# Row sums of one head of four, in two query chunks of every odd attention step, taken on VectorE instead of ScalarE

## The chip, the cores and the metric

One core of a Trainium2 chip runs the whole kernel. The metric is the device time of one execution in microseconds. The kernel before took 660.53 us (median of 3 runs, 660.41 to 660.67).

## The reference

The input `x` is (8, 512, 512): 8 batches of 512 tokens with 512 features. There are 16 heads of 32 features. A conditioning token per batch goes through the same projections and is added to the queries and keys, and the attention's output is added to `x`:

```python
Q = split_heads(x @ Wq.T + bq)
K = split_heads(x @ Wk.T + bk)
V = split_heads(x @ Wv.T + bv)
tQ = split_heads(tokens @ Wq.T + bq)
tK = split_heads(tokens @ Wk.T + bk)
scores = einsum('bhqd,bhkd->bhqk', Q + tQ, K + tK) / sqrt(32)
attn = softmax(scores, axis=-1)
out = einsum('bhqk,bhkd->bhqd', attn, V)
return x + out            # heads put side by side again
```

Everything is in float32. A softmax row needs its largest score, the exponentials of the 512 scores less that largest one, and the sum of these exponentials. This sum, one number for each query and head, is what the change is about.

## The kernel before

**Steps.** A step `t` is one batch and one group of four heads: 8 batches with 4 groups give 32 steps. The 512 queries (and keys) are four chunks of 128. The main loop (L1133) runs over steps 1 to 28; the first step and the last three are written out ahead of it and behind it.

**Two kinds of steps.** Weighting the values needs exponentials with the keys on the partitions. The row maxima and row sums are made with the queries on the partitions.

- In *odd* steps 1 to 27 (`BLOCKED`, L76) the exponentials that are made query-wise for the sums are kept. `denominators` (L679) writes them into eight rooms of a ring called `arena` (`rows_kept`, L222), four rooms for the first two query chunks and four for the other two. In a room the four heads of a chunk stand side by side, so one head of one chunk is four pieces of 128 columns, one in each of four rooms. `exchange` (L668) moves them between partitions by DMA, 16 transfers for each half (12 from SP's queue, 4 from GpSimd's), into `blocks`. `turn_blocks` (L661) transposes them on VectorE in 32x32 blocks. They are then keyed and go straight into the weighted sum (`times_v`, L765).
- In *even* steps the query-wise exponentials are thrown away (written back over the scores in PSUM), only their sums are kept, and `exponentials` (L744) makes the scores again key-wise, with the row maximum subtracted by a first matmul (L749), and then the exponentials (L763, ScalarE) into the other rooms of `arena`.

**One pass of the loop.** Step `t` has four items, called V, q, k and v. In each item

1. if `t` is even, `exponentials(t, i)` makes the keyed exponentials of key chunk `i`: matmuls L749 and L752, then four ScalarE instructions L763;
2. `row_max` (L606) makes the scores of a query chunk of the *next* step, four heads, each in a PSUM bank (matmuls L646, or L638 in odd steps), and VectorE takes their maxima (L602 for one head, L655 for two). In items V, q and k these are chunks 1, 2 and 3 of step `t + 1`; in item v it is chunk 0 of step `t + 2`;
3. `denominators` (L679) makes the four exponentials of that chunk on ScalarE (L693), one for each head, with the row maximum as bias. Each also asks for the sum of what it makes (`accum_out`). The profile shows such a sum as an instruction of its own behind the exponential, an ACTIVATION_READ_ACCUMULATOR on the same line;
4. the item's own product: in V the weighted sum of step `t - 1` (L774), in q, k and v part of the projections of the next batch (matmuls L469). The projections are multiplied block by block in seven products instead of eight. In even steps an item makes three of the seven (`three_products`, L547), and VectorE adds them up in three instructions, L556, L557 and L558, straight out of two PSUM banks. In odd steps an item makes four of them (`four_products`, L517), which ScalarE (L540 to L543) and GpSimd (L544, L545) take up.

So the query-wise exponentials of an odd step are made one step earlier, in the even one: chunk 1 in item V, chunk 2 in item q, chunk 3 in item k.

**Order and banks.** Each engine's order is written out by hand: a manual schedule takes the instructions of an engine in the order in which the code names them. PSUM has eight banks. `released` (L144) writes down, item by item, which of them come free in which order, and `begin` (L137) hands them out again. In an even step the scores of an item go into four banks: two that held scores of the item before, free when ScalarE has made the exponentials from them, and two that held its product, free when VectorE has done L557 and L558. In item k, for example, the scores L646 wait for the third and fourth head's exponentials of item q and for L557 and L558 of item q.

**Where the sums go.** `masked` (L794, GpSimd L801) takes a step's sums in that step's own item k, TensorE spreads them over the partitions (L811), and VectorE takes reciprocals (L821) that scale the weighted values.

Of the kernel before, what the change touches and what calls it, by code (L numbers as in the profile page):

```python
# [12 lines left out]
ALU = mybir.AluOpType  # L13
AX = mybir.AxisListType
# [3 lines left out]
def kernel(  # L18
# [38 lines left out]
    nc = tc.nc  # L57
# [14 lines left out]
    EARLY = 3  # L72
    SINGLY = "qk"
    BY_POOL = (3,)
    WARM = (48, 4)
    BLOCKED = list(range(1, T - 4, 2))  # L76

# [44 lines left out]
    def banks(i, n=1):  # L122

        row = row_of[0] or [at_end[j] for j in TURNS[turn[0]]]
        j = row[i]
        if n == 1:
            return psum[:, j, :]
        k = row[i + 1]
        return psum[:, j : k + 1 : k - j, :]
# [7 lines left out]
    def begin(w):  # L137
        rows = order[w : w + 4]
        pairs = [(j, j + 1) for j in rows if j + 1 in rows]
        last = max(pairs, key=lambda p: rows.index(p[0]) + rows.index(p[1]), default=sorted(rows[2:]))  # L140
        order[w : w + 4] = sorted(j for j in rows if j not in last) + list(last)
        row_of[0] = list(order)

    def released(*roles):  # L144
        order[:] = [row_of[0][i] for i in roles]
# [76 lines left out]
    def rows_kept(t, half):  # L222

        a = arena[:, half * HG : (half + 1) * HG, :]
        return a.rearrange("p g (c h s) -> p g c h s", c=2, h=HG)
# [368 lines left out]
    sums = {}  # L594
# [66 lines left out]
    def turn_blocks(t, units):  # L661

        for n in units:
            pr = slice(n % NP * 2, n % NP * 2 + 2)
            e = blocked[t][:, :, n // NP, pr, :].rearrange("p g h s -> p g (h s)")
            nc.vector.transpose(e, e)  # L666

    def exchange(t, half):  # L668
# [3 lines left out]
        for g in range(HG):  # L672
            for a in range(HG):
                queue = nc.gpsimd if a in BY_POOL else nc.sync
                of = arena[a * BL : (a + 1) * BL, half * HG + g, :]
# [3 lines left out]
    def denominators(t, qc, w=HG, js=range(HG)):  # L679

        if t >= T - 2:
            return
        for j in js:
            if t in BLOCKED:
                to = rows_kept(t, qc // 2)[:, :, qc % 2, j, :].rearrange(
                    "p g (c e) -> p g c e", e=BL
                )
            else:
                to = banks(w + j)
            of = banks(w + j)  # L690
            if t in BLOCKED:
                of = of.rearrange("p (c g e) -> p g c e", g=HG, e=BL)
            nc.scalar.activation(  # L693
                to,
                of,
                AF.Exp,
                bias=nmax[t][:, qc, j, :],
                accum_out=sums[t][:, qc, j, :],
            )

    def split_max(t, on=nc.gpsimd):

        if t >= T or t in BLOCKED:
            return
        m, sp = nmax[t], split[t % 2]
        rest = op.tile([P, NS, HG, 1], F32, tag="rest", name=f"rest_{t}")
        on.tensor_copy(sp[:, :, :, 0:1], m)
        on.tensor_tensor(rest, m, sp[:, :, :, 0:1], ALU.subtract)
        on.tensor_copy(sp[:, :, :, 1:2], rest)
        on.tensor_tensor(sp[:, :, :, 2:3], rest, sp[:, :, :, 1:2], ALU.subtract)  # L710
# [7 lines left out]
    def turn_max(t):  # L718

        if t >= T or t in BLOCKED:  # L720
            return
        maxT[t] = room_for_max(t)
        nc.sync.dma_start_transpose(
            maxT[t].rearrange("p (c q) -> p c q", c=NS),
            split[t % 2].rearrange("p c h e -> p (c h e)"),
        )
# [17 lines left out]
    def exponentials(t, kc, at=None):  # L744

        bank = [bank_of(i) for i in at] if at else [banks(i) for i in range(HG)]
        for j in range(HG):
            r = slice(j * HD, j * HD + 3)
            nc.tensor.matmul(bank[j], onesb[r, :], maxT[t][r, :], start=True, stop=False)  # L749
        for j in range(HG):  # L750
            r = slice(j * HD, (j + 1) * HD)
            nc.tensor.matmul(  # L752
                bank[j],
                qkT["k", t][r, kc * P : (kc + 1) * P],
                qkT["q", t][r, :],
                start=False,
                stop=True,
            )
        for pr in range(NP):
            e = room_for_e(t, kc, pr)  # L760
            es[t, kc, pr] = e
            for i in range(2):
                nc.scalar.activation(e[:, i, :], bank[pr * 2 + i], AF.Exp)  # L763
# [145 lines left out]
    def keep_warm(n):  # L909
        for _ in range(n):  # L910
            nc.tensor.matmul(warm[:, :P], onesb, onesb, start=True, stop=True)

    keep_warm(WARM[0])
    bank = bank_of
# [5 lines left out]
    def turn_first_x(half):  # L920
        if half == 0:
            xT[0] = xtp.tile([P, NC, S], F32, tag="xT", name="xT_0")
        for cs in ((slice(0, 1), slice(1, 2)) if half else (slice(0, 2),)) + (slice(2, 4),):
            nc.vector.transpose(
                xT[0][:, cs, two[half]].rearrange("p c (f i) -> p c f i", i=BL),
                x0[:, half_of_x[half], cs, :].rearrange("p f c e -> p c f e"),
            )

    def project(t, n, pt, at=slice(0, S)):
        for cc in range(NC):  # L930
            project_qk_part(t, n, cc, pt, at)
# [5 lines left out]
    project(0, "k", pk, two[0])  # L937
    keep_warm(WARM[1])
    turn_first_x(1)
# [156 lines left out]
    def products(t, n, blocks, hold, dens, small):  # L1096

        b, r = (t - 1) // G + 1, (t - 1) % G
        hold()
        if r % 2:  # L1100
            three_products(n, b, r // 2, dens, small, (0, 3))
            released(1, 2, 4, 5, 6, 7, 0, 3)
        elif blocks:
            four_products(n, b, r // 2, dens, small, 4)
            released(6, 7, 0, 1, 2, 3, 5, 4)
        else:
            four_products(n, b, r // 2, dens, small, 0)
            released(2, 3, 4, 5, 6, 7, 1, 0)
# [5 lines left out]
    def turn_more(t, i):  # L1114

        for u in (t - 1, t, t + 1):
            if u in BLOCKED and (t - u, i) in TURNED:
                n = turned.get(u, 0)
                turned[u] = n + TURNED[t - u, i]
                turn_blocks(u, range(n, turned[u]))  # L1120

    ORDERS = {
        (1, 0): [],
        (1, 1): ["store", "x"],
# [8 lines left out]
    for t in range(1, T - 3):  # L1133
        b, r = divmod(t, G)
        blocks = t in BLOCKED
        w = 0 if blocks else HG
        items = ["V", "q", "k", "v"]
        for i, item in enumerate(items):
            rows = (t + 1, i + 1) if i < 3 else (t + 2, 0)
            begin(w)  # L1140
            if not blocks:
                exponentials(t, i)
            late_first = item in ("v" if blocks else "qkv") and t % 2 == 1
            hold = row_max(*rows, late_first, w, not blocks and item in SINGLY)

            def held(i=i, hold=hold):
                hold()
                if i == 2:
                    split_max(t + 1)
                    turn_max(t + 1)  # L1150

            dens = lambda js=range(HG): denominators(*rows, w, js)
            if item in "qkv":
                products(t, item, blocks, held, dens, nothing)
            else:
                held()
                dens()
                if blocks:
                    weighted(t - 1, banks(4), banks(5), nothing)
                    released(6, 7, 0, 1, 2, 3, 5, 4)  # L1160
                else:
                    weighted(t - 1, banks(0), banks(1), nothing)
                    released(2, 3, 1, 4, 5, 6, 7, 0)
            if i == 0 and r % 2 == 0:
                turn_x(t + NC + 2)
                turn_x(t + NC + 3)
            if i == 0 and r == 1:
                combine_x(b + 1, 1, nc.gpsimd)
            if i == 1 and r == 0:
                combine_x(b + 1, 0, nc.gpsimd)  # L1170
            if i == 2:
                aparts[t] = masked(t)
            turn_more(t, i)
            for what in ORDERS[t % 2, i]:
                if what == "store":
                    store()
                elif what == "residual":
                    if 3 < t + 1 <= T - 4:
                        load_residual(t + 1)
                elif what == "x":  # L1180
                    load_pairs()
                elif t + 1 in BLOCKED:
                    exchange(t + 1, what)
# [67 lines left out]
    t = T - 3  # L1251
# [25 lines left out]
    t = T - 2  # L1277
# [25 lines left out]
    t = T - 1  # L1303
# [117 lines left out]
```

## Time and profile before

| | |
|---|---|
| median of 3 runs | 660.53 us (660.41 to 660.67) |
| the profiled execution's own time | 660.98 us |
| its span, first to last instruction | 658.9 us |
| TensorE busy | 651.5 us, granted clock 1.00 |
| VectorE busy | 574.6 us |
| ScalarE busy | 542.5 us |
| GpSimd busy | 336.8 us |
| query-wise exponentials that are kept (L693) | 224, with 224 reads of the accumulator |
| query-wise exponentials that are not kept (L693) | 256, with as many reads |

The profile is of one execution. PE is TensorE's matmuls, PEld its weight loads, DVE is VectorE, ACT ScalarE, POOL GpSimd and SP the engine that only issues DMAs. In rows in order of time the columns are start, duration, engine, line, operation, the tile written and the tile read, shapes, how many instructions were merged into the row, and, in square brackets, how long the engine stood idle before it and what ended that. In rows of groups they are line, engine, operation, tiles, shapes and count, then busy time and mean duration in ns of one, then the idle time before them. Instructions of one engine overlap a little: the next starts before the end of the last is written, so the distance between two starts is shorter than a duration. A float32 matmul is two passes with a weight load each, so one row of scores for four heads is eight matmuls.

### The profile page before, as it was taken

Reading aid. Unit: us, or ns where it says so; the run is one execution under the profiler, and the core shown is the slowest. Engines: PE = TensorE matmul, PEld = TensorE weight load, DVE = VectorE, ACT = ScalarE, POOL = GpSimd, SP = SyncE. Lnnn points to the kernel's source line nnn. Section 1 sums busy time; section 2 is a strip of 40 time slices with the busy share of each in tenths; the row PEclk is TensorE's granted clock in tenths of the full one; section 3 lists DMA queues with packets and bytes.
Section 4 is the critical chain, followed back from the end, with each engine's and each line's share of the span. In section 5 each row is a group of like instructions: output and inputs, shape, how many; then the busy total and the mean of one; then the engine's idle time right before and its main releaser. Section 6 shows DMA issues by size and latency. Waiting matters only on the chain.

```text
span 658.9 us, 23947 instructions
## 1 busy us (share of the span) xinstructions
PE 651.5 (99%) x9568; PEld 304.1 (46%) x9568; DVE 574.6 (87%) x844; ACT 542.5 (82%) x1393; POOL 336.8 (51%) x446
## 2 busy tenths in 40 slices
PE   8999999999999999999999999999999999999997
PEld 7444443544535454444445444454553544444432
DVE  4898989989798898979989898898979888897886
ACT  2579798888989888898989979788897988889664
POOL 5552543647537464466635664464753646444340
PEclk9999999999999999999999999999999999999999
DMA  9718548385675838657484875839567582940212
GB/s 205 144 44 214 118 109 210 67 220 122 153 172 121 209 74 214 149 130 194 94 214 97 191 155 131 210 71 217 118 164 166 115 205 48 223 106 4 56 33 33
DMA packets 140818, 90.91 MB, mean 138 GB/s; under 512 B 117436, under 2 KB 126308, under 8 KB 140708
## 3 DMA queue, kind: packets, MB, share of 16 engines
q1 hardware_dynamic: 133252, 73.91, 49.0%
q0 software_dynamic: 5568, 14.95, 8.8%
q8 instruction: 75, 1.23, 0.8%
q10 hardware_dynamic: 1888, 0.52, 0.4%
q14 instruction: 35, 0.29, 0.1%
HBM read 20.27 MB, written 8.39 MB: 43 GB/s over the span
## 4 chain that ended last, share of the span: by engine, by line
PE 95%; POOL 2%; DVE 1%; DMA 1%; issue 0%; ACT 0%; ACTq 0%; DVEq 0%; POOLq 0%
PE psum L469 43%; PE psum L774 17%; PE psum L646 10%; PE psum L638 9%; PE psum L752 8%; PE psum L749 3%; PE psum L410 2%; DMA early<-in_x_dram 1%; PE psum L1227 1%; PE psum L1340 0%; PE psum L811 0%; ACT psum L693 0%; POOL wc_q L364 0%; POOL wc_q L361 0%; POOL wc_k L362 0%
## 5 line engine op out<-in xcount | busy, mean ns | idle before, releaser
L602 DVE TENSOR_REDUCE nmax<-psum 128x1 f32<-128x512 f32 x326 | 204.9, 680 | 41.7 <-PE psum L646 38.2
L693 ACT ACTIVATE psum<-psum,nmax 128x512 f32<-128x512 f32 x256 | 169.2, 665 | 46.5 <-DVE nmax L602 34.3
L763 ACT ACTIVATE arena<-psum 128x512 f32<-128x512 f32 x264 | 136.3, 603 | 29.3 <-PE psum L752 21.7
L693 ACT ACTIVATE arena<-psum,nmax 128x512 f32<-128x512 f32 x224 | 152.8, 709 | 5.8 <-issue 4.4
L666 DVE STREAM_TRANSPOSE blocks<-blocks 128x1024 f32<-128x1024 f32 x112 | 132.2, 1218 | 0.2 <-issue 0.2
L655 DVE TENSOR_REDUCE nmax<-psum 128x2 f32<-128x1024 f32 x87 | 105.3, 1212 | 1.1 <-PE psum L646 1.1
L842 POOL TENSOR_TENSOR res<-res,recs 128x512 f32<-128x512 f32 x30 | 31.4, 1048 | 121.1 <-DVE res L841 121.1
L677 POOL DMA_DIRECT2D blocks<-arena x112 | 55.9, 504 | 72.3 <-ACT arena L693 63.5
L646 PE MATMUL psum<-kT,qT 32*128 32x512 f32 x576 | 87.9, 604 | 0.0
L774 PE MATMUL psum<-arena,v 128*32 128x512 f32 x576 | 68.5, 597 | 0.0
L752 PE MATMUL psum<-qT,kT 32*128 32x512 f32 x528 | 67.9, 587 | 0.0
L638 PE MATMUL psum<-kT,qT 32*64 32x512 f32 x896 | 62.4, 613 | 0.0
L646 PEld LDWEIGHTS psum<-kT,qT 32*128 32x128 f32 x576 | 37.6, 182 | 34.1 <-DVE kT L558 6.5
L693 ACT ACTIVATION_READ_ACCUMULATOR psum<-psum,nmax 128x1 f32 x256 | 52.4, 205 | 0.0
L774 PE MATMUL psum<-blocks,v 128*32 128x256 f32 x896 | 52.1, 381 | 0.0
L693 ACT ACTIVATION_READ_ACCUMULATOR arena<-psum,nmax 128x1 f32 x224 | 50.9, 227 | 0.0
L843 POOL TENSOR_TENSOR xr<-res,xr 128x512 f32<-128x512 f32 x30 | 38.4, 1281 | 2.4
L209 POOL TENSOR_TENSOR xr<-xr,wT_q 128x512 f32<-128x512 f32 x30 | 38.3, 1280 | 0.3
L774 PEld LDWEIGHTS psum<-blocks,v 128*32 128x32 f32 x896 | 26.3, 110 | 25.0 <-ACT arena L763 10.6
L841 DVE STREAM_TRANSPOSE res<-psum 128x512 f32<-128x512 f32 x28 | 20.1, 717 | 19.0 <-issue 16.0
L469 PE MATMUL psum<-wT_v,xT 128*32 128x256 f32 x512 | 34.2, 382 | 0.0
L469 PE MATMUL psum<-wc_v,xc 128*32 128x256 f32 x512 | 33.5, 379 | 0.0
(194 smaller groups left out, 1012.3 us busy)
## 6 DMA issues: line engine op xcount, KB each, us to landing
blocks<-arena SPq DMA_DIRECT2D x336, 128.0 KB, 4.1
blocks<-arena POOLq DMA_DIRECT2D x112, 128.0 KB, 4.0
xr<-in_x_dram SPq DMA_DIRECT2D x60, 128.0 KB, 2.8
x<-in_x_dram SPq DMA_DIRECT2D x56, 128.0 KB, 2.8
out_dram<-xr SPq DMA_DIRECT2D x56, 128.0 KB, 2.3
w_q<-in_L_cond_Wq_dram SPq DMA_DIRECT2D x4, 256.0 KB
w_k<-in_L_cond_Wk_dram SPq DMA_DIRECT2D x4, 256.0 KB, 8.2
w_v<-in_L_cond_Wv_dram SPq DMA_DIRECT2D x4, 256.0 KB
```

Source lines behind the costliest of these rows:

```text
L469: nc.tensor.matmul(pt[r], still[:, r], moving, start=(kc == kcs[0]), stop=(kc == kcs[-1]))
L602: nc.vector.tensor_reduce(nmax[t][:, qc, j : j + 1, 0], pt, AX.X, ALU.max, negate=True)
L638: nc.tensor.matmul(pt[i * n : (i + 1) * n], qkT["q", t][r, qc * P + i * n : qc * P + (i + 1) * n], qkT["k", t][r, :], start=True, stop=True,)
L646: nc.tensor.matmul(pt, qkT["q", t][r, qc * P : (qc + 1) * P], qkT["k", t][r, :], start=True, stop=True,)
L655: nc.vector.tensor_reduce(nmax[t][:, qc, pr * 2 : pr * 2 + 2, 0], pt, AX.X, ALU.max, negate=True)
L666: nc.vector.transpose(e, e)
L677: queue.dma_start(to.rearrange("p c h s -> p (c h s)"), of)
L693: nc.scalar.activation(to, of, AF.Exp, bias=nmax[t][:, qc, j, :], accum_out=sums[t][:, qc, j, :],)
L752: nc.tensor.matmul(bank[j], qkT["k", t][r, kc * P : (kc + 1) * P], qkT["q", t][r, :], start=False, stop=True,)
L763: nc.scalar.activation(e[:, i, :], bank[pr * 2 + i], AF.Exp)
L774: nc.tensor.matmul(pt[j * HD : (j + 1) * HD, at], vs[b % 2][:, kc, (g * HG + j) * HD : (g * HG + j + 1) * HD], e, start=(kc == chunks[0]), ...
L843: nc.gpsimd.tensor_tensor(xr[t], y, xr[t], ALU.add)
```

## The change

For steps 3 to 27 (odd), the exponentials of head 0 in query chunks 2 and 3 are made without `accum_out`. VectorE adds up the kept exponentials instead, with one `tensor_reduce` for each of the two chunks, right behind the product of items q and k of the even step before. Step 1 keeps all its sums on ScalarE. That is 13 odd steps with two sums each.

```diff
+    BY_VECTOR = {2:(0,),3:(0,)}
...
             of = banks(w + j)
             if t in BLOCKED:
                 of = of.rearrange("p (c g e) -> p g c e", g=HG, e=BL)
+            by_scalar = t not in BLOCKED or t == 1 or j not in BY_VECTOR.get(qc, ())
             nc.scalar.activation(
                 to,
                 of,
                 AF.Exp,
                 bias=nmax[t][:, qc, j, :],
-                accum_out=sums[t][:, qc, j, :],
+                **({"accum_out": sums[t][:, qc, j, :]} if by_scalar else {}),
             )
+
+    def sums_by_vector(t, qc):
+
+        if t in BLOCKED:
+            for j in BY_VECTOR[qc]:
+                nc.vector.tensor_reduce(
+                    sums[t][:, qc, j, :],
+                    rows_kept(t, qc // 2)[:, :, qc % 2, j, :],
+                    AX.XY,
+                    ALU.add,
+                )
...
+    SUMMED = {1:[2],2:[3]}
...
             turn_more(t, i)
+            if not blocks:
+                for qc in SUMMED.get(i, ()):
+                    sums_by_vector(t + 1, qc)
             for what in ORDERS[t % 2, i]:
```

## The prediction, made before the changed kernel ran

> **What bounds the kernel now.** I read the page first (busy shares, then the chain that ended last), then one pair of steps by windows, then the order of time of TensorE, its weight loads, ScalarE and VectorE inside one even step.
>
> ```profile
> span 658.9 us, 23947 instructions
> ...
> PE 651.5 (99%) x9568; PEld 304.1 (46%) x9568; DVE 574.6 (87%) x844; ACT 542.5 (82%) x1393; POOL 336.8 (51%) x446
> ...
> PE 95%; POOL 2%; DVE 1%; DMA 1%; issue 0%; ACT 0%; ACTq 0%; DVEq 0%; POOLq 0%
> ```
>
> TensorE is busy 99% and is 95% of the chain. So what the change does to ScalarE or VectorE counts only where TensorE waits for one of them. One odd and one even step together, from one max of row scores to the same one two steps on, take 39.04 us:
>
> ```profile
> core 0: us, PE busy (x) PEld busy (x) DVE busy (x) ACT busy (x) POOL busy (x), PEclk, DMA share, GB/s
> 301.46:340.50 39.04, 39.04 (x600) 18.06 (x592) 35.09 (x51) 33.89 (x88) 21.24 (x28) 1.00 0.65 153
> ```
>
> VectorE and ScalarE have some 4 and 5 us free in each such pair, TensorE none. The question is where TensorE is stretched. The same eight matmuls of row scores (L646) stand in items q, k and v of the even step:
>
> ```profile
> 324.84 1.02 PE L646 MATMUL psum<-kT,qT 32*128 32x512 f32 x8
> ...
> 329.61 1.33 PE L646 MATMUL psum<-kT,qT 32*128 32x512 f32 x8
> ...
> 334.70 1.02 PE L646 MATMUL psum<-kT,qT 32*128 32x512 f32 x8
> ```
>
> In items q and v they take 1.02 us, in item k 1.33: 0.31 us lost in each even step. That is the one place near the change where TensorE visibly stands. Its weight loads say why:
>
> ```profile
> 329.36 0.76 PEld L646 LDWEIGHTS psum<-kT,qT 32*128 32x128 f32 x8 [0.41 <-DVE qT L557]
> ...
> 329.82 0.30 PEld L646 LDWEIGHTS psum<-kT,qT 32*128 32x128 f32 x4
> ```
>
> The second row is the same view begun at 329.81: two of the four heads' loads do not start before 329.82. The view names VectorE's L557, but that is the release of the first load alone. What lets the late loads go is found by laying the other two engines beside them:
>
> ```profile
> 325.04 2.06 ACT L763 ACTIVATE arena<-psum 128x512 f32<-128x512 f32 x4 [0.89 <-PE psum L752]
> 326.96 0.71 ACT L693 ACTIVATE arena<-psum,nmax 128x512 f32<-128x512 f32 x1
> 327.53 0.23 ACT L693 ACTIVATION_READ_ACCUMULATOR arena<-psum,nmax 128x1 f32 x1
> 327.62 0.72 ACT L693 ACTIVATE arena<-psum,nmax 128x512 f32<-128x512 f32 x1
> ...
> 328.95 0.73 ACT L693 ACTIVATE arena<-psum,nmax 128x512 f32<-128x512 f32 x1
> 329.52 0.25 ACT L693 ACTIVATION_READ_ACCUMULATOR arena<-psum,nmax 128x1 f32 x1
> 329.81 2.06 ACT L763 ACTIVATE arena<-psum 128x512 f32<-128x512 f32 x4
> 331.73 0.71 ACT L693 ACTIVATE arena<-psum,nmax 128x512 f32<-128x512 f32 x1
> ```
>
> ```profile
> 328.63 0.68 DVE L557 TENSOR_TENSOR qT<-psum,qT 128x512 f32<-128x512 f32 x1
> 329.22 0.41 DVE L558 TENSOR_TENSOR qT<-psum,qT 128x256 f32<-128x256 f32 x1
> 330.67 2.48 DVE L602 TENSOR_REDUCE nmax<-psum 128x1 f32<-128x512 f32 x4 [1.03 <-PE psum L646]
> ...
> 334.00 0.41 DVE L558 TENSOR_TENSOR kT<-psum,kT 128x256 f32<-128x256 f32 x1
> 335.75 1.29 DVE L602 TENSOR_REDUCE nmax<-psum 128x1 f32<-128x512 f32 x2 [1.34 <-PE psum L646]
> ```
>
> L557 ends at 328.63 + 0.68 = 329.31, and the first load follows at 329.36: 0.05 us from an end to what it releases. L558 ends at 329.63, so it would have let its load go at 329.68. ScalarE's last read of its accumulator ends at 329.52 + 0.25 = 329.77, and 0.05 later is 329.82. So the last bank is given free by ScalarE: the fourth head's row exponentials of item q, counted to the end of their accumulator read.
>
> **The change part by part.**
>
> *ScalarE, 26 accumulator reads go* (13 even steps, chunks 2 and 3, one head each). A head now takes 327.62 − 326.96 = 0.66 us from start to start: 0.57 until its read, 0.09 for the read. The exponential alone, with its bias from memory and no accumulator, is not in the trace. The nearest rows are these:
>
> ```profile
> 313.81 0.71 ACT L542 ACTIVATE kT<-psum,tok 128x512 f32<-128x512 f32 x1
> 314.39 0.49 ACT L543 ACTIVATE kT<-psum,aparttok 128x256 f32<-128x256 f32 x1
> ...
> L763 ACT ACTIVATE arena<-psum 128x512 f32<-128x512 f32 x264 | 136.3, 603 | 29.3 <-PE psum L752 21.7 <-ACT arena L693 5.0 <-issue 1.0
> L693 ACT ACTIVATE arena<-psum,nmax 128x512 f32<-128x512 f32 x224 | 152.8, 709 | 5.8 <-issue 4.4
> ```
>
> L542 has a bias from memory, no accumulator and the duration of L693 (0.71): the next instruction starts 0.58 after it. L763 has no such bias: four take 2.06 (row of 329.81), so one follows the other after (2.06 − 0.60)/3 = 0.49. So the saving of a head is 0.08 (by L542), 0.09 (the read alone) or at most 0.17 (by L763). I take 0.09, the bias being what L693 and L542 share. There is a rule for this: the Trainium skill, "ScalarE: Activation LUTs", section "What ACT_TABLE_LOAD costs", gives an ACTIVATE with a bias from memory 280 ns + 0.833 ns an element, less 93 ns of overlap, so an estimate of 0.61 us at 512; by that the saving would be 0.05, the whole sum 0.6 us and the time 659.9. The rows disagree with it (0.57 and 0.58), and they decide.
>
> The saved head is the first of the four, and ScalarE runs without idle from 325.04 to 329.77, so the other three move forward whole. Item q: the last read ends at 329.68, the late load goes at 329.73 instead of 329.82. VectorE's gate (329.68) is just ahead of that. TensorE gains 0.09 of its 0.31. Nothing more follows on ScalarE: L763 of item k starts at 329.81 as before, because it waits for TensorE's L752, which stands ahead of the stretch.
>
> *Item v must keep up*, or the gain is lost there:
>
> ```profile
> 334.46 0.31 PEld L646 LDWEIGHTS psum<-kT,qT 32*128 32x128 f32 x4 [0.43 <-DVE kT L558]
> ...
> 334.29 0.25 ACT L693 ACTIVATION_READ_ACCUMULATOR arena<-psum,nmax 128x1 f32 x1
> 334.94 1.57 ACT L763 ACTIVATE arena<-psum 128x512 f32<-128x512 f32 x3 [0.40 <-ACT arena L693]
> ```
>
> Its last bank is free at 334.29 + 0.25 + 0.05 = 334.59, some 0.11 ahead of the matmuls at 334.70. In item k the matmuls lost 0.31 with loads 0.21 late, so a load seems to be wanted about 0.10 early: item v has no slack left. TensorE arrives 0.09 sooner, and the read taken from chunk 3 brings ScalarE forward by the same 0.09. So the gain passes, no more. What ScalarE saves in item k otherwise falls into its idle 0.40.
>
> *VectorE, 26 sums are added*, each the next instruction after L558 of items q and k. A sum over 128x512 from SBUF is not in the trace; near it stand these:
>
> ```profile
> L602 DVE TENSOR_REDUCE nmax<-psum 128x1 f32<-128x512 f32 x326 | 204.9, 680 | 41.7 <-PE psum L646 38.2 <-PE psum L638 2.8
> L655 DVE TENSOR_REDUCE nmax<-psum 128x2 f32<-128x1024 f32 x87 | 105.3, 1212 | 1.1 <-PE psum L646 1.1
> L376 DVE STREAM_TRANSPOSE xT<-x 128x512 f32<-128x512 f32 x28 | 17.8, 673 | 0.0
> ```
>
> Four L602 take 2.48, so one costs (2.48 − 0.68)/3 = 0.60 of VectorE's time, 0.68 to its end. I take 0.60; ends 0.60 (as in PSUM) and 1.21 (if four pieces of 128 cost as twice the elements). It waits for its own head's exponential alone, ended at 327.67 and 332.44; VectorE comes to it at 329.6 and 334.4, so the wait costs nothing. Behind it stands L602 of the next item, which itself waits for TensorE: 1.03 and 1.34 idle, 0.94 and 1.25 once TensorE comes 0.09 sooner. A sum of 0.60 (15.6 us in all) vanishes in these gaps. The cover is gone from 0.94 on. No queue, DMA or TensorE instruction is moved; the sums are read by GpSimd most of a step later.
>
> *Sum.* 13 even steps (t = 2 to 26). One of them is already disturbed:
>
> ```profile
> 323.94 0.72 DVE L841 STREAM_TRANSPOSE res<-psum 128x512 f32<-128x512 f32 x1 [1.12 <-issue]
> ...
> 519.51 0.72 DVE L841 STREAM_TRANSPOSE res<-psum 128x512 f32<-128x512 f32 x1 [1.47 <-issue]
> ```
>
> The first row is the usual step, the second that of t = 24: VectorE starts L841 0.35 later, so TensorE is late in item k and the bank is free in time; I count nothing there. 12 × 0.09 = 1.1 us. The profiled execution took 660.98 us (span 658.9 and 2.1 around it), the median of the three runs is 660.53, so 0.45 less; the saving is the same in both: 659.9 for the profiled one, 659.4 for the median.
>
> **Rivals.**
>
> *Nothing reaches the end (660.5).* For it: the waits view gives the 13 waits of this place to VectorE, and VectorE's gate lies only 0.14 before ScalarE's.
>
> ```profile
> PEld psum L646 <- ACT arena L693: 6.4, 27, 0.2
> PEld psum L646 <- DVE qT L557: 5.2, 13, 0.4
> ```
>
> Against it: the late load follows ScalarE's end by the 0.05 seen elsewhere.
>
> *More is saved (658.8).* If an exponential without accumulator follows as closely as L763 does, ScalarE saves up to 0.17, and TensorE gains until VectorE's gate: 329.82 − 329.68 = 0.14, times 12, 1.7 us. Against it: L542.
>
> *Slower.* The sum holds up VectorE. Place: L602 of item k, then L556 to L558, whose end opens the first load of item v (334.46, about 0.13 before it is needed). It decides from a sum of 0.94 + 0.13 = 1.07 us on; at the upper end of 1.21 it takes 0.14 × 13 = 1.8 us against the 1.1 gained, 661.2, and from 1.16 on the kernel is slower than before; at 1.5 us a sum the loss is 5.6, the time 665.0. For it: VectorE is the second busiest engine, at 87%, and the reading of four separate pieces is unmeasured. Against it: every VectorE row of 512 elements lies between 0.67 and 0.72. The Trainium skill, "Perfetto Trace Analysis", section "Optimizing Scalar/DVE Operations", speaks for this side: it would move work from VectorE to ScalarE when VectorE is the full one. Here the idle 1.03 and 1.34 at the very place speak against applying it.
>
> That the change does not do what it says is excluded: in the built program VectorE has 26 instructions more, 26 exponentials have lost their sum, and the order on the other engines is unchanged.
>
> **How the numbers follow.** Forecast 0.64 (659.4, its own range 659.0 to 659.9); nothing 0.14; more 0.13; slower 0.09. The range runs from 658.7 (more, less 0.1 of run to run) to 660.7 (nothing, plus 0.2 of it), which leaves out the slower case and little else. A measurement tells about 0.2% here, 1.3 us: below 659.2 or above 661.85. The forecast's 1.1 us lies just inside. Faster: all of "more" and about a third of the forecast, 0.35. Same: the rest of the forecast and "nothing", 0.57. Slower: 0.08, since a sum that passes 1.16 at all would hardly stop short of 1.26, where 661.85 is reached.
>
> **What would show it.** L646 in item k takes 1.24 instead of 1.33, still 1.02 in items q and v; a pair of steps takes 38.95; ScalarE's first head in chunks 2 and 3 is followed after 0.57; VectorE's new line takes about 0.68 in groups, and the idle before L602 shrinks to some 0.3 and 0.6 without L602 starting later relative to TensorE. The forecast is wrong if L646 stays at 1.33, if the new line takes over 1 us, or if the 0.09 gained in item k reappears as a stretched L646 in item v.

## The result, and the profile after

| | before | after |
|---|---|---|
| median of ten runs each, side by side | 660.57 us (660.23 to 660.98) | 658.82 us (658.30 to 659.38) |
| ratio, 95% interval | | 0.9975 (0.9967 to 0.9983) |
| the profiled execution | 660.98 us | 659.38 us |

The changed kernel is faster by 1.75 us, 0.25% (0.17 to 0.33%). The forecast was 659.4 in a range from 658.7 to 660.7.

The diff moves the lines: the rows L602, L646, L693, L763 and L841 of before are L603, L647, L695, L776 and L854 of after, and the new sum is L707. First the page of after: span, busy times, and the chain that ended last by engine.

```profile
span 657.6 us, 23947 instructions
...
PE 648.9 (99%) x9568; PEld 301.1 (46%) x9568; DVE 589.9 (90%) x870; ACT 540.2 (82%) x1367; POOL 336.8 (51%) x446
...
PE 93%; SPq 2%; POOL 2%; DMA 1%; DVE 1%; issue 0%; ACTq 0%; POOLq 0%; DVEq 0%
```

VectorE is busy 15.3 us longer, TensorE 2.6 us shorter, and TensorE still sets the end. The pair of steps that took 39.04 is the second fence, from the same max of row scores to the one two steps on (from:to and length, then busy time and instructions of TensorE, its loads, VectorE, ScalarE and GpSimd):

```profile
301.18:340.13 38.95, 38.95 (x600) 17.91 (x592) 36.27 (x53) 33.72 (x86) 21.21 (x28) 1.00 0.66 155
```

It is 0.09 shorter. Inside it, in order of time, the row scores of items V, q, k and v on TensorE:

```profile
318.73 1.16 PE L647 MATMUL psum<-kT,qT 32*128 32x512 f32 x8
...
324.56 1.02 PE L647 MATMUL psum<-kT,qT 32*128 32x512 f32 x8
...
329.33 1.24 PE L647 MATMUL psum<-kT,qT 32*128 32x512 f32 x8
...
334.33 1.02 PE L647 MATMUL psum<-kT,qT 32*128 32x512 f32 x8
```

Item k fell from 1.33 to 1.24, and items q and v stayed at 1.02. On ScalarE, the first and the last row of item q's exponentials:

```profile
326.68 1.29 ACT L695 ACTIVATE arena<-psum,nmax 128x512 f32<-128x512 f32 x2
...
329.14 0.26 ACT L695 ACTIVATION_READ_ACCUMULATOR arena<-psum,nmax 128x1 f32 x1
```

The first row holds two exponentials, because no accumulator read stands between them any more. The second alone takes 0.72 (the row of 327.62 in the prediction), so it follows the first after 1.29 − 0.72 = 0.57. The last read ends at 329.40, 0.07 after the start of item k's matmuls; in before it ended 0.16 after it (329.77 and 329.61). These 0.09 are the gain. The late weight loads follow that end by 0.05, as in before. This is the view of the weight loads begun at 329.53:

```profile
329.45 0.30 PEld L647 LDWEIGHTS psum<-kT,qT 32*128 32x128 f32 x4
```

VectorE's own release would have let them go at 329.40 (L559 ends at 328.94 + 0.41 = 329.35). And on VectorE:

```profile
328.94 0.41 DVE L559 TENSOR_TENSOR qT<-psum,qT 128x256 f32<-128x256 f32 x1
329.28 0.67 DVE L707 TENSOR_REDUCE sums<-arena 128x1 f32<-128x512 f32 x1
330.39 2.48 DVE L603 TENSOR_REDUCE nmax<-psum 128x1 f32<-128x512 f32 x4 [0.44 <-PE psum L647]
...
334.05 0.67 DVE L707 TENSOR_REDUCE sums<-arena 128x1 f32<-128x512 f32 x1
335.38 1.29 DVE L603 TENSOR_REDUCE nmax<-psum 128x1 f32<-128x512 f32 x2 [0.66 <-PE psum L647]
```

The sums lie in the idle time ahead of L603: 0.44 and 0.66 of it are left, and L603 still waits for TensorE, 1.06 after the start of its matmuls (330.39 − 329.33) as before (330.67 − 329.61). The groups say the same of the whole kernel (busy time, mean ns of one, idle time before):

```profile
L603 DVE TENSOR_REDUCE nmax<-psum 128x1 f32<-128x512 f32 x326 | 204.8, 679 | 25.3 <-PE psum L647 21.7 <-PE psum L639 2.8
...
L695 ACT ACTIVATION_READ_ACCUMULATOR arena<-psum,nmax 128x1 f32 x198 | 45.0, 227 | 0.0
...
L707 DVE TENSOR_REDUCE sums<-arena 128x1 f32<-128x512 f32 x26 | 17.5, 673 | 0.0
```

Idle before the maxima was 41.7 and is 25.3. The 16.4 us that went are about what 26 sums need at 0.60 from start to start (15.6).

**Where the time came from.** The loop can be measured from the row scores in item V of t = 1 to those in item V of t = 27, thirteen pairs of steps on TensorE, each with one even step (t = 2 to 26). In before, these are the first, the two around t = 24, and the last:

```profile
64.98 1.11 PE L638 MATMUL psum<-kT,qT 32*64 32x512 f32 x16
...
494.55 1.11 PE L638 MATMUL psum<-kT,qT 32*64 32x512 f32 x16
...
533.92 1.11 PE L638 MATMUL psum<-kT,qT 32*64 32x512 f32 x16
...
572.97 1.11 PE L638 MATMUL psum<-kT,qT 32*64 32x512 f32 x16
```

And the same four in after:

```profile
65.16 1.11 PE L639 MATMUL psum<-kT,qT 32*64 32x512 f32 x16
...
493.81 1.11 PE L639 MATMUL psum<-kT,qT 32*64 32x512 f32 x16
...
532.76 1.11 PE L639 MATMUL psum<-kT,qT 32*64 32x512 f32 x16
...
571.72 1.11 PE L639 MATMUL psum<-kT,qT 32*64 32x512 f32 x16
```

The loop went from 507.99 to 506.56, 1.43 less. The pair of t = 24 alone went from 39.37 to 38.95, 0.42 of it. Of the other twelve the first pair is 39.14 and 39.15, and eleven went from 39.04 or 39.05 to 38.94 to 38.96, together 1.0. Outside the loop, after's execution lost 0.18 ahead of it and won some 0.3 around the span (660.98 − 658.9 = 2.1 against 659.38 − 657.6 = 1.8): 1.6 in all, the difference of the two executions.

So the mechanism gives about 1.0 in those eleven pairs, and t = 24 gives 0.4, of which 0.1 is the same mechanism (below). The 0.3 that the medians show beyond these 1.4 lies within the noise: 0.17 to 0.33% is 1.1 to 2.2 us. The pair lengths below are worked out in this way from each kernel's own trace.

### The profile page after: what moved, and what is told of

The parts are those of the page before. It is cut to its first block, busy times and chain, and to the rows that moved or that the text cites. A ratio compares the mean times of both kernels' runs of the same rounds, so it can differ in the third digit from the quotient of the medians.

```text
span 657.6 us, 23947 instructions
## 1 busy us (share of the span) xinstructions
PE 648.9 (99%) x9568; PEld 301.1 (46%) x9568; DVE 589.9 (90%) x870; ACT 540.2 (82%) x1367; POOL 336.8 (51%) x446
## 4 chain that ended last, share of the span: by engine, by line
PE 93%; SPq 2%; POOL 2%; DMA 1%; DVE 1%; issue 0%; ACTq 0%; POOLq 0%; DVEq 0%
PE psum L470 43%; PE psum L787 18%; PE psum L647 10%; PE psum L639 9%; PE psum L765 9%; PE psum L762 3%; SPq L255 2%; DMA x<-in_x_dram 1%; PE psum L1244 1%; DMA early<-in_x_dram 1%; PE psum L1357 0%; PE psum L824 0%; SPq L170 0%; POOL wc_k L363 0%; POOL wc_k L365 0%
## 5 line engine op out<-in xcount | busy, mean ns | idle before, releaser
L603 DVE TENSOR_REDUCE nmax<-psum 128x1 f32<-128x512 f32 x326 | 204.8, 679 | 25.3 <-PE psum L647 21.7
L695 ACT ACTIVATE psum<-psum,nmax 128x512 f32<-128x512 f32 x256 | 169.2, 665 | 46.4 <-DVE nmax L603 34.1
L776 ACT ACTIVATE arena<-psum 128x512 f32<-128x512 f32 x264 | 136.3, 603 | 30.4 <-PE psum L765 21.4
L695 ACT ACTIVATE arena<-psum,nmax 128x512 f32<-128x512 f32 x224 | 150.4, 709 | 5.7 <-issue 4.4
L647 PE MATMUL psum<-kT,qT 32*128 32x512 f32 x576 | 86.4, 604 | 0.0
L695 ACT ACTIVATION_READ_ACCUMULATOR psum<-psum,nmax 128x1 f32 x256 | 52.5, 205 | 0.0
L647 PEld LDWEIGHTS psum<-kT,qT 32*128 32x128 f32 x576 | 35.5, 182 | 34.8 <-DVE kT L559 7.4
L695 ACT ACTIVATION_READ_ACCUMULATOR arena<-psum,nmax 128x1 f32 x198 | 45.0, 227 | 0.0
L854 DVE STREAM_TRANSPOSE res<-psum 128x512 f32<-128x512 f32 x28 | 20.1, 717 | 18.8 <-issue 15.7
```

Source lines behind the costliest of these rows:

```text
L603: nc.vector.tensor_reduce(nmax[t][:, qc, j : j + 1, 0], pt, AX.X, ALU.max, negate=True)
L647: nc.tensor.matmul(pt, qkT["q", t][r, qc * P : (qc + 1) * P], qkT["k", t][r, :], start=True, stop=True,)
L695: nc.scalar.activation(to, of, AF.Exp, bias=nmax[t][:, qc, j, :], **({"accum_out": sums[t][:, qc, j, :]} if by_scalar else {}),)
```

## The experiments

The theory: ScalarE's accumulator read is the last thing that holds item k's bank, so a read less in chunk 2 is worth 0.09 there, a read less in chunk 3 keeps it from being lost in item v, and VectorE's sums cost nothing. The rivals: each chunk brings half by itself; the sums cost something that a larger saving covers; the 0.4 at t = 24 has nothing to do with it. All kernels below are timed against before in five rounds. The ratios can differ a little from the quotient of the medians beside them.

**One chunk alone.** Only chunk 2's head is summed by VectorE, then only chunk 3's.

```diff
-    BY_VECTOR = {2:(0,),3:(0,)}
+    BY_VECTOR = {2:(0,)}
...
-    SUMMED = {1:[2],2:[3]}
+    SUMMED = {1:[2]}
```

> Only chunk 2's sum of the first head goes to VectorE. Theory (a bank is freed 0.09 us sooner in item k, and item v has no slack unless its own read goes too): the scores of item k take 1.24 us as in the changed kernel, those of item v grow from 1.02 to about 1.11, a pair of steps stays at 39.04 us, and the time is that of before, 660.5 (660.2 if the single late transpose of t = 24 is absent). Rival (each read that goes is worth the same, wherever it stands): half the gain, a pair of 39.00, 659.7.

```diff
-    BY_VECTOR = {2:(0,),3:(0,)}
+    BY_VECTOR = {3:(0,)}
...
-    SUMMED = {1:[2],2:[3]}
+    SUMMED = {2:[3]}
```

> Only chunk 3's sum of the first head goes to VectorE. Theory: item k's scores stay at 1.33 us, item v's at 1.02, the pair at 39.04, the time at 660.5 (660.2 if the late transpose is absent). Rival (each read is worth the same): a pair of 39.00, 659.7.

Measured: chunk 2 alone 660.78 against 660.58 (0.9999, 0.9990 to 1.0008), chunk 3 alone 660.66 against 660.58 (1.0001, 0.9992 to 1.0010). Items k and v of the step, first in the order of time of chunk 2 alone:

```profile
329.14 1.24 PE L647 MATMUL psum<-kT,qT 32*128 32x512 f32 x8
...
334.13 1.11 PE L647 MATMUL psum<-kT,qT 32*128 32x512 f32 x8
```

and then of chunk 3 alone:

```profile
329.87 1.34 PE L647 MATMUL psum<-kT,qT 32*128 32x512 f32 x8
...
334.95 1.02 PE L647 MATMUL psum<-kT,qT 32*128 32x512 f32 x8
```

The first gains 0.09 in item k and loses 0.09 in item v; the second gains nothing anywhere. Pairs take 39.04 and 39.05, as before. Neither half is worth anything by itself, so the rival of half a gain each falls.

**The sums alone.** ScalarE keeps all its sums, and VectorE makes its 26 as well, into a tile that nobody reads.

```diff
+    spare = const.tile([P, 2, 1], F32, tag="spare", name="spare")
...
-            by_scalar = t not in BLOCKED or t == 1 or j not in BY_VECTOR.get(qc, ())
+            by_scalar = True
...
-                    sums[t][:, qc, j, :],
+                    spare[:, qc - 2, j : j + 1],
```

> ScalarE keeps all its sums; VectorE makes the 26 sums as well, into a tile that nothing reads. Theory (the sums lie in VectorE's idle time and TensorE's stretch is ScalarE's doing): the pair stays at 39.04, the time at 660.5, or 660.2 if the late transpose of t = 24 goes with the moved instructions. Rival (the sums cost something that the saved reads outweigh): above 660.8. Second rival (what was gained beyond the forecast comes from the longer VectorE program): 659.9 or less.

Measured: 662.74 against 660.58, 1.0035 (1.0022 to 1.0047), 2.2 us slower, by the time alone the side of the rival (above 660.8). But the loop was not slower: pairs took 39.05, and the first row scores of the loop began at 68.12 instead of 64.98. All of it lay ahead of the loop, where no such sum runs. So the tile, not the sums, came under suspicion, and the experiment was made again without `spare`, the sums written into a tile that was there already:

```diff
-                    spare[:, qc - 2, j : j + 1],
+                    table,
```

> As vector_adds (ScalarE keeps all its sums, VectorE makes the 26 sums as well and nothing reads them), but into a tile that the kernel has anyway, so that no tile changes its address. In vector_adds the pair of steps stayed at 39.04 us and all of the added 2 us lay ahead of 45 us, where every DMA took longer. Theory (the extra tile of 8 bytes a partition moved the others, the sums themselves cost nothing): 660.5, a pair of 39.04, x loads at 2.8 us to landing again. Rival (26 more instructions on VectorE slow the start by themselves): 662.7 again.

Measured: 660.17 against 660.54, 0.9996 (0.9987 to 1.0005). VectorE in this kernel, item q's sum and the maxima of item k:

```profile
329.52 0.67 DVE L707 TENSOR_REDUCE table<-arena 128x1 f32<-128x512 f32 x1
330.63 2.48 DVE L603 TENSOR_REDUCE nmax<-psum 128x1 f32<-128x512 f32 x4 [0.44 <-PE psum L647]
```

Item k took 1.34, the pairs 39.05: the sums neither cost nor bring anything. The pair of t = 24 takes 39.05 here as well, so of its 0.42 the late transpose that is gone gives 0.32 and the saved reads 0.1.

**The tile alone.** The kernel before, with that tile of 8 bytes a partition set to zero once, and nothing else.

```diff
+    spare = const.tile([P, 2, 1], F32, tag="spare", name="spare")
+    nc.vector.memset(spare, 0.0)
```

> The kernel before with one unused tile of 8 bytes a partition added in front of the other tiles, set to zero once; nothing else. Theory (the address of the tiles alone slows every DMA, as in vector_adds): 662.7, x loads at 3.4 us to landing, the pair at 39.04. Rival (it was the sums written there): 660.5, x loads at 2.8.

Measured: 663.33 against 660.83, 1.0042 (1.0029 to 1.0054); pairs of 39.05, and the loop's first row scores at 67.34. The DMA view (KB each, median us from issue to landing), first of before and then of this kernel:

```profile
blocks<-arena SPq DMA_DIRECT2D x336, 128.0 KB, 4.1
...
x<-in_x_dram SPq DMA_DIRECT2D x56, 128.0 KB, 2.8
...
w_k<-in_L_cond_Wk_dram SPq DMA_DIRECT2D x4, 256.0 KB, 8.2
```

```profile
blocks<-arena SPq DMA_DIRECT2D x336, 128.0 KB, 4.1
...
x<-in_x_dram SPq DMA_DIRECT2D x56, 128.0 KB, 3.4
...
w_k<-in_L_cond_Wk_dram SPq DMA_DIRECT2D x4, 256.0 KB, 9.5
```

With these eight bytes a partition the loads from DRAM are slower, and ahead of the loop TensorE waits for them: VectorE's transpose L342 stands idle 2.77 for the load of `w_k` instead of 1.29, and TensorE's matmuls behind it 2.08 instead of 0.48. The exchange between partitions (`blocks<-arena`) is as fast as ever. It is not the memset, which the first kernel with this tile does not have, and its loads of `x` take the same 3.4. That the tile acts by shifting the tiles behind it is likely, but not shown: no run shows the addresses.

**ScalarE's half alone.** The 26 sums are left out altogether: ScalarE does not make them, and VectorE writes the constant 256 in their place.

```diff
-                nc.vector.tensor_reduce(
-                    sums[t][:, qc, j, :],
-                    rows_kept(t, qc // 2)[:, :, qc % 2, j, :],
-                    AX.XY,
-                    ALU.add,
-                )
+                nc.vector.memset(sums[t][:, qc, j, :], 256.0)
```

> The 26 sums are left out on ScalarE, and VectorE writes a constant in their place (the sums of these heads are left out). Theory: the same as the changed kernel, a pair of 38.95 and 658.8, since VectorE's sums cost nothing. Rival (the sums cost something): faster than the changed kernel by what they cost, 658.3 or less.

Measured: 658.83 against 660.58, 0.9969 (0.9957 to 0.9982), pairs of 38.96. Its VectorE at item q's end:

```profile
328.54 0.06 DVE L707 MEMSET sums<- 128x1 f32 x1
329.62 2.48 DVE L603 TENSOR_REDUCE nmax<-psum 128x1 f32<-128x512 f32 x4 [1.02 <-PE psum L647]
```

The gap of 1.02 is back, and the kernel is no faster than the one that fills it. What is gained is ScalarE's, and the sums ride along at no cost.

**Chunk 0 too, and alone.** In item V the row scores take 1.16, and there too ScalarE's end lies late. In the order of time of before, its copy in front of item V's matmuls (which begin at 319.01) is this:

```profile
318.39 0.61 ACT L532 COPY v<-psum 128x512 f32<-128x512 f32 x1
```

It ends at 319.00, where in item v an end 0.16 ahead of the matmuls (334.54 against 334.70) was just enough. So chunk 0 of the odd step, whose exponentials come shortly before that copy, should be worth another 0.09.

```diff
-    BY_VECTOR = {2:(0,),3:(0,)}
+    BY_VECTOR = {0:(0,),2:(0,),3:(0,)}
...
+                if not blocks and 0 in BY_VECTOR:
+                    sums_by_vector(t + 1, 0)
```

> The changed kernel, with the sum of the first head of chunk 0 on VectorE as well, placed ahead of the weighted sum's end in item V of the even step, where VectorE stands idle for 1.12 us. Theory (a read that goes is worth 0.09 us where a bank freed by ScalarE holds TensorE up): in item V the scores wait for ScalarE's copy L532, which ends the same run of instructions as the four exponentials of chunk 0; its scores go from 1.16 to 1.07 us, a pair from 38.95 to 38.86, the time to 657.7. Rival (ScalarE there is held by VectorE's maxima, so the saved read is lost in a wait): a pair of 38.95, 658.8.

Chunk 0 alone has `BY_VECTOR = {0:(0,)}` and `SUMMED = {}`, with the same two lines added.

> Only chunk 0's sum of the first head goes to VectorE. Theory: item V's scores 1.07, items q, k and v as before (1.02, 1.33, 1.02), a pair of 38.95, 659.4. Rival (item V's gain is lost at the next place, or was VectorE's): a pair of 39.04, 660.5.

Measured: 658.11 against 660.54, 0.9963 (0.9950 to 0.9977), with all three; 659.92 against 660.54, 0.9993 (0.9984 to 1.0001), with chunk 0 alone, whose gain rests on the pairs, as its interval holds 1. Item V takes 1.10 in both, not 1.07, and pairs take 38.89 and 38.98. In the first of them, ScalarE's exponentials of the first two heads and VectorE's maxima ahead of them:

```profile
314.33 1.34 ACT L695 ACTIVATE arena<-psum,nmax 128x512 f32<-128x512 f32 x2 [0.31 <-DVE nmax L603]
```

```profile
313.60 2.48 DVE L603 TENSOR_REDUCE nmax<-psum 128x1 f32<-128x512 f32 x4
```

In item V the exponentials follow close on the maxima. The second alone lasts about 0.69, so it begins at 314.98, 0.65 after the first and not 0.57. The maxima are 0.60 apart, the second ends at 313.60 + 0.60 + 0.68 = 314.88, and with the read gone ScalarE has caught up with it. In before the two were 0.67 apart (315.25 and 315.92), so this spacing saves 0.02; the rest of the 0.06 seems to come from the first exponential, which starts 0.73 after the start of the maxima instead of 0.78 (315.25 against 314.47). Why it does, no run shows. So the first head seems the wrong one to spare here; that is argued from the times, and the next kernel tests it.

**Chunk 0 with its second head.** VectorE sums the second head, so ScalarE stays behind the maxima as before.

```diff
-    BY_VECTOR = {2:(0,),3:(0,)}
+    BY_VECTOR = {0:(1,),2:(0,),3:(0,)}
...
+                if not blocks and 0 in BY_VECTOR:
+                    sums_by_vector(t + 1, 0)
```

> As chunk0_too, but in chunk 0 it is the second head's sum that goes to VectorE instead of the first's. In chunk0_too item V's scores took 1.10 us instead of the expected 1.07: the second exponential there waited for VectorE's second maximum, so of 0.09 only 0.07 was saved. Theory: the read behind the second head is followed by an exponential whose maximum is long there, so all 0.09 is saved: item V 1.07, a pair of 38.86, 657.7. Rival (the next instruction waits for something too): 38.89, 658.1.

Measured: 658.02 against 660.83, 0.9958 (0.9946 to 0.9970), the best of all. Items V, k and v in its order of time:

```profile
317.71 1.07 PE L647 MATMUL psum<-kT,qT 32*128 32x512 f32 x8
...
328.23 1.25 PE L647 MATMUL psum<-kT,qT 32*128 32x512 f32 x8
...
333.23 1.02 PE L647 MATMUL psum<-kT,qT 32*128 32x512 f32 x8
```

Item V falls to 1.07 and a pair to 38.87: the whole 0.09. Its interval and that of the changed kernel overlap, so only that it beats before is measured by time; that it beats the changed kernel rests on the pairs, 0.08 each.

**Two heads in chunks 2 and 3.** This fills the gap of VectorE to the brim, and looks for the point at which the sums begin to cost.

```diff
-    BY_VECTOR = {2:(0,),3:(0,)}
+    BY_VECTOR = {2:(0,1),3:(0,1)}
```

> Two heads' sums instead of one in chunks 2 and 3 go to VectorE. Theory: in item k ScalarE's bank comes 0.18 us sooner, so VectorE's own gate (end of L558) holds TensorE: item k's scores 1.20; but two sums take 1.26 of VectorE's time where 0.94 is idle, so its maxima of item k start about 0.2 late and item v's scores grow to about 1.09: a pair of 38.98 to 39.0, slower than the changed kernel by 0.4 to 0.6 us, 659.3. Rival (VectorE has room, ScalarE is all that matters): a pair of 38.91, 658.3. Second rival (VectorE's lateness is carried on and grows): above 660.5.

Measured: 660.11 against 660.54, 0.9993 (0.9985 to 1.0002). VectorE at items q and k of a step that nothing else disturbs:

```profile
368.64 1.27 DVE L707 TENSOR_REDUCE sums<-arena 128x1 f32<-128x512 f32 x2
369.82 2.47 DVE L603 TENSOR_REDUCE nmax<-psum 128x1 f32<-128x512 f32 x4
```

and TensorE at items k and v of it:

```profile
368.69 1.21 PE L647 MATMUL psum<-kT,qT 32*128 32x512 f32 x8
...
373.65 1.10 PE L647 MATMUL psum<-kT,qT 32*128 32x512 f32 x8
```

No idle time is left before L603. Item k gains no more than 0.12, since VectorE's own release is next in line (L559 ends at 368.71, and the last loads go at 368.77), and item v loses 0.08, since the maxima of item k, and with them L557 to L559, come later. A pair takes 39.00: of the gain half is left. Three pairs took longer, 0.7 in all, nearly what the time lacks to the 659.3 of the theory (0.8). In two of them (39.32 and 39.27) L854 starts late, as in before at t = 24; in the third (39.12) it is ScalarE's L776 in item v that does, with 0.72 idle ahead of it against 0.46 in the pair before.

**The step t = 24, once more.** Both kernels were run unchanged a second time.

> The kernel before, unchanged, profiled a second time. Theory (one late transpose of 0.33 us falls in some executions, at no fixed step): 660.5, twelve or thirteen pairs of 39.04 and the late one gone or at another step than t = 24. Rival (it belongs to this program, and its absence is part of what the change gained): again late at t = 24.

> The changed kernel, unchanged, timed and profiled a second time. Theory: pairs of 38.95, 1.1 us less in the loop than before, a time of 659.0 with what differs ahead of the loop from run to run; a late transpose may show in one step. Rival (more is gained than the loop shows): 658.5 or less with no late transpose in the profile of before.

Measured: before 660.81 against 660.83 (1.0000, 0.9991 to 1.0008), after 659.22 against 660.83 (0.9975, 0.9965 to 0.9985). The second profile of before has the late transpose at the same step:

```profile
519.84 0.72 DVE L841 STREAM_TRANSPOSE res<-psum 128x512 f32<-128x512 f32 x1 [1.48 <-issue]
```

and in both profiles of after that step looks like any other; this is the first:

```profile
518.43 0.72 DVE L854 STREAM_TRANSPOSE res<-psum 128x512 f32<-128x512 f32 x1 [1.12 <-issue]
```

So the theory, that the delay falls at no fixed step, is wrong, and the rival holds: the delay belongs to the program and not to one execution, as far as two profiles of each kernel show. In chunk 2 alone, chunk 3 alone and chunk 0 alone the sixth pair is 0.3 longer (39.33, 39.35 and 39.28). There the transpose is on time, and another VectorE instruction is late, the first maximum in item k of t = 11. In chunk 2 alone:

```profile
270.38 1.29 DVE L603 TENSOR_REDUCE nmax<-psum 128x1 f32<-128x512 f32 x2 [0.36 <-PE psum L639]
```

One pair earlier it has no idle time ahead of it. The sums alone, ScalarE's half alone, both kernels with three chunks and the tile alone have no such pair. What the engine waits for in these 0.3 to 0.4 us the views do not show. One thing goes with it: the DMA records of the kept traces have some 35 packets of 8 KB in a queue that the DMA view calls `q14 instruction`, and one of them starts 0.7 to 1.4 us behind each of the eight late starts found in these six profiles. So the engine may stand there between two blocks of its program, whose borders a change of the kernel shifts. No run tests this, and it stays open.

## Why the prediction was right

The time lay within 0.6 us of the forecast and inside the range, and L646 in item k, the pair and the first head came out as listed under what would show it. By its steps:

- *The last bank of item k is given free by ScalarE's accumulator read.* That ScalarE gives it free is shown: with one read less ahead of it the row scores take 1.24 or 1.25, with or without VectorE's sum (chunk 2 alone, ScalarE's half alone), and 1.34 with it (the sums alone). That it is the end of the fourth head's read, and not of its exponential, rests on the 0.05 from that end to the late loads (329.77 and 329.82 in before, 329.40 and 329.45 in after); no run takes that read away.
- *A head saves 0.09.* Right: the first head is followed after 0.57, against 0.66. The Trainium skill's formula, which gave an estimate of 0.61 and a time of 659.9, is not what this exponential does ("ScalarE: Activation LUTs", section "What ACT_TABLE_LOAD costs"). The rival that it follows as closely as L763 (0.49) falls by the same row.
- *Item v keeps up only because chunk 3's read goes too.* Shown by chunk 2 alone, where item v gives the 0.09 back (1.11).
- *The sums hide in VectorE's idle time.* Shown by the sums alone. A sum takes 0.67 to its end, so four separate pieces of 128 in SBUF cost no more than one row in PSUM, and the slower rival falls. Its argument that every VectorE row of 512 elements lies between 0.67 and 0.72 was not quite so: in before two with three operands (L494) take 0.73 and 0.75, and one transpose (L1324) 0.65. One more number was off: of the 1.03 before item k's maxima I left 0.94, as TensorE would come sooner. It does not in item k: L603 waits for the first head's scores, which were never late. The gap stays 1.02 (ScalarE's half alone), of which 0.44 was left. Two heads show the other side: at 1.18 (369.82 − 368.64) the gap is full, and the loss of 0.08 in item v is near the 0.11 that the prediction's point of 1.07 gives.
- *Twelve pairs by 0.09.* Eleven of these twelve, in fact: in the first pair item k falls too (1.25 to 1.16), but item v's scores start only 0.03 sooner for it and take 1.14 instead of 1.10, and all is lost again. That is 1.0 instead of 1.1.
- *Nothing at t = 24.* This is the term that was mis-sized. It brought 0.42: 0.32 because the late transpose is gone from that step, and 0.1 because item k, no longer late for that reason, gains there as elsewhere. Rows of its items q, k and v in before, then in after:

```profile
520.06 1.36 PE L646 MATMUL psum<-kT,qT 32*128 32x512 f32 x8
...
525.17 1.07 PE L646 MATMUL psum<-kT,qT 32*128 32x512 f32 x8
...
530.02 1.25 PE L646 MATMUL psum<-kT,qT 32*128 32x512 f32 x8
```

```profile
519.32 1.03 PE L647 MATMUL psum<-kT,qT 32*128 32x512 f32 x8
...
524.10 1.24 PE L647 MATMUL psum<-kT,qT 32*128 32x512 f32 x8
...
529.08 1.02 PE L647 MATMUL psum<-kT,qT 32*128 32x512 f32 x8
```

The prediction was right that item k is not held up there (1.07), but took the delay as something that stays. It went away with the change, as it did with other changes of the kernel, and says nothing for or against the mechanism. That makes up the larger part of what the forecast missed; what is left is within the noise.

## What to carry to other kernels

An accumulator read on ScalarE takes 0.09 us of the engine's time here and delays the release of every bank behind it in ScalarE's order, so it counts where TensorE's weight load waits for such a release, even with ScalarE idle 18% of the time. Look for the stretched matmul first, name the engine whose end comes 0.05 before the late load, and then check the next item: a gain passes on only if its own gate moves by as much (chunk 2 alone brought nothing). Which head gives up its sum matters too, since a head ahead of one that waits for its maximum saves less (0.06 instead of 0.09).

## What the runs showed of the hardware

- A tile of 8 bytes a partition ahead of the others slowed the loads from DRAM (2.8 to 3.4 us, 8.2 to 9.5) and cost the kernel 2.5 us, 0.42% (0.29 to 0.54), more than the change gained. The traces show the slower landings, not what in them takes longer. The Trainium skill, "Collectives: The Full Stack", section "Rules for kernel authors", wants buffers of collectives aligned to 32 bytes, against a hardware read-modify-write; these loads are no collectives, but a shift of 8 bytes would fall under such a rule. That this is the reason no run here shows; other shifts were not tried.
- VectorE can start an instruction some 0.35 us late with nothing in the profile that it waits for (idle 1.47 against 1.12), at a step that depends on the program. Here it cost 0.32 in one pair, about what four pairs gain by the change. All eight late starts found, one of them ScalarE's, lie 0.7 to 1.4 us ahead of an 8 KB packet of the instruction queue; that the two are connected is not shown.
- An accumulator read moves what stands behind it on ScalarE by 0.09 us: an exponential of 128x512 is followed after 0.57 without it and 0.66 with it. TensorE's late weight loads came 0.05 us after the end of the last read.
